# A conditional block's first sequences copied in DRAM, updated there by indirect transfers, and loaded once

## The chip, the cores and the metric

The kernel runs on one core of a Trainium2 chip. A core has five engines that run side by side, each with its own instruction stream: TensorE (PE, matrix products), VectorE (DVE), ScalarE (ACT), GpSimd (POOL) and SyncE (SP, which here only issues DMA transfers). Sixteen DMA engines move the data; transfers are issued from the queues of SP, ACT and POOL. The metric is the device time of one launch in microseconds (us).

## The reference

The input is `x` (32 sequences of 128 tokens of 512 features, float32), a conditioning vector per sequence, and a mask that is true only at the tail of a sequence (0 to 32 of its 128 tokens).

```python
shift, scale, gate_msa = jnp.split(_silu(t) @ ada_w + ada_b, 3, axis=1)
norm = _layernorm(x) * (1.0 + scale[:, None]) + shift[:, None]
norm = jnp.where(m, norm, 0.0)
fwd = _ssm_fallback(norm, ssm_w1, ssm_b1, ssm_w2, ssm_b2)   # gelu(u @ w1 + b1) @ w2 + b2
bwd = ...                                                   # the same with bwd_*, token by token
x = x + gate_msa[:, None] * jnp.where(m, fwd + bwd, 0.0)
shift_mlp, scale_mlp, gate_mlp = jnp.split(_silu(t) @ ffada_w + ffada_b, 3, axis=1)
ff_norm = _layernorm(x) * (1.0 + scale_mlp[:, None]) + shift_mlp[:, None]
h = _gelu(ff_norm @ ff_w1 + ff_b1)                          # 512 -> 1024
return x + gate_mlp[:, None] * (h @ ff_w2 + ff_b2)
```

The first half changes only masked tokens, some 512 of the 4096. The second half is a feed-forward layer over all tokens.

## The kernel before, in words

**Slots.** The masked tokens are numbered in order; these numbers are slots. The kernel finds the token of each slot on the chip (`find_slots`, `tokens_of`), gathers the rows of `x` for 512 slots, 128 at a time, into the tiles `xc` (`gather_slots`, L232), and runs the first half on these rows alone, in two parts of 256 slots. For each part it modulates (L167, L168), transposes on PE and copies the result with ACT (`transposed_slots`, L175, L176), multiplies by the first weights with a Gelu on ACT (`hidden`, L184, L188), and multiplies by the second (`project`, L198). `finish_slots` adds the bias, multiplies by the gate, adds the slot's row of x (L200, L201, L289) and stores 128 finished rows to a DRAM buffer `x1_rows` (L290). The hidden steps and projects of the first part are called "s0", of the second "s1"; the four finishes are numbered 0 to 3.

**Pairs.** The second half takes the sequences in four pairs of sides; a side is 4 sequences, a pair is 1024 tokens. The x of a pair is loaded by four transfers of two sequences each (`load_side`, L319). Then `take_first_half` (L656) overwrites the masked tokens' rows in these tiles by eight indirect transfers from `x1_rows`, issued by POOL, one for each sequence. For each token the statistics are taken (`Statistics`, L688, L689; the root is POOL's L694), x is normalised (L700), transposed to features by rows, and scaled and shifted (`scale_and_shift`: L708 on DVE, L710 on ACT). In the first pair, side 0 is transposed in blocks of 32 by DVE (L1132) and by 16 transfers that put the blocks in place, 8 from SP's queue and 8 from ACT's (`turned`, L727); side 1 is transposed by PE (`transposed`, L716) in four groups called turn(0) to turn(3), which stand between and behind the matmuls of project "s3".

**Seven products instead of eight.** Both feed-forward products are done by a recursive block scheme with seven block products, P1 to P7, in place of eight. It needs sums and differences of blocks: of tokens (`TokenBlocks.one(1..4)`, L757; `token_sums`, L817 to L827, all on DVE), and of weights. `weight_sums(1..4)` (L577) forms the combinations of ff_w1 on DVE, in two buffers that they use in turn: the tiles `spare`, which later hold x of the second pair, for 1 and 3, and `t_2` for 2 and 4. Each is stored to the DRAM buffer `t_rows` by transfers from SP's queue (L579, L581, L582); the product loads them as `tw` when it needs them (L834). `fw2_of.combine(0..3)` (L308) forms combinations of ff_w2. `FirstProduct` works through outer products 1, 2, 5, 6, 3, 7, 4; its matmuls are L888, `seed` (L932 on DVE, L934 on ACT) prepares an accumulator with earlier results, and P6, P7 and P4 end with additions on DVE (L913, L918, L923), some also with POOL's additions L939, L968 and L972. `SecondProduct` follows (L1068).

**What sets the order.** The whole part up to L1320 is a manual schedule: every engine runs its instructions exactly in the order of the program text, and waits only at semaphores. So a step that waits holds back all that its engine has behind it. Around the change the program is: first part of slots, `weight_sums(1)` and (2), finish 0, the "s3" transposes, finish 1, the modulation of the second half (`mod2`, its transposes L618, `modT` L621), `weight_sums(3)` and (4), then the first pair's x, "s1", and finishes 2 and 3. Finishes 2 and 3 belong to slots of later pairs.

The tile pool `xp` has eight places: two `xc` pairs, two `spare` and the four x tiles of a pair.

## Time and profile before

| | |
|---|---|
| time, median of 3 runs | 470.43 us (468.70 to 472.58) |
| the profiled execution's own time | 470.92 us |
| its span, first to last instruction | 469.2 us |
| PE busy | 452.4 us (96%), 2000 matmuls |
| DVE busy | 334.0 us (71%), 538 instructions |
| ACT busy | 174.9 us (37%) |
| POOL busy | 159.4 us (34%) |
| granted TensorE clock, mean | 0.995 |
| moved by DMA | 70.41 MB, mean 150 GB/s |

Busy time doesn't tell what bounds a stage; waits and the order of time do. A timeline line has the start, the duration, the engine, the line of the program, what is written and read, and in brackets how long the engine was idle before it and what ended that. A line of waits has the total, the number and the longest. A line of the stages has the busy time of PE, PE's weight loads, DVE, ACT and POOL (with the instructions in brackets), then the granted clock, the busy share of the DMA engines and their GB/s.

### The profile page before, as it was taken

Reading aid. Unit: us, or ns where it says so; the run is one execution under the profiler, and the core shown is the slowest. Engines: PE = TensorE matmul, PEld = TensorE weight load, DVE = VectorE, ACT = ScalarE, POOL = GpSimd, SP = SyncE. Lnnn points to the kernel's source line nnn. Section 1 sums busy time; section 2 is a strip of 40 time slices with the busy share of each in tenths; the row PEclk is TensorE's granted clock in tenths of the full one; section 3 lists DMA queues with packets and bytes.
Section 4 is the critical chain, followed back from the end, with each engine's and each line's share of the span. In section 5 each row is a group of like instructions: output and inputs, shape, how many; then the busy total and the mean of one; then the engine's idle time right before and its main releaser. Section 6 shows DMA issues by size and latency. Waiting matters only on the chain.

```text
span 469.2 us, 5826 instructions
## 1 busy us (share of the span) xinstructions
PE 452.4 (96%) x2000; PEld 365.3 (78%) x2000; DVE 334.0 (71%) x538; ACT 174.9 (37%) x380; POOL 159.4 (34%) x151
## 2 busy tenths in 40 slices
PE   6899999897999999999999999999999999999995
PEld 2475384475878888888888888888888888888884
DVE  4649377999778966997687498967873995434645
ACT  3131022543365074153643712545537134462000
POOL 6200063046876000189740003897100024660000
PEclk9999999999999999999999999999999999999999
DMA  8999943490413861854068528240863341213012
GB/s 278 386 408 362 394 172 53 86 345 19 121 44 134 137 90 49 312 174 163 1 194 106 106 98 288 102 161 3 217 100 88 125 168 62 96 64 117 0 76 107
DMA packets 82194, 70.41 MB, mean 150 GB/s; under 512 B 63136, under 2 KB 63664, under 8 KB 81138
## 3 DMA queue, kind: packets, MB, share of 16 engines
q1 hardware_dynamic: 67298, 57.95, 40.1%
q0 software_dynamic: 4256, 10.75, 6.8%
q10 hardware_dynamic: 10608, 1.32, 2.0%
q8 instruction: 17, 0.28, 0.2%
q14 instruction: 15, 0.12, 0.1%
HBM read 56.83 MB, written 13.17 MB: 149 GB/s over the span
## 4 chain that ended last, share of the span: by engine, by line
PE 61%; POOL 6%; ACT 6%; DVE 5%; issue 2%; POOLq 0%; DVEq 0%
PE a_o L1068 18%; PE e_o L1068 16%; PE a_m L888 14%; PE e_m L888 12%; ACT hb L850 2%; POOL hb L972 2%; ACT ha L850 1%; POOL ha L972 1%; POOL ha L939 1%; POOL rstd L694 1%; DVE xT L827 1%; PE last L1068 1%; DVE sx L817 1%; ACT a_o L1014 1%; ACT e_o L1014 1%
## 5 line engine op out<-in xcount | busy, mean ns | idle before, releaser
L939 POOL TENSOR_TENSOR ha<-p_m,ha 128x512 f32<-128x512 f32 x20 | 27.2, 1361 | 152.7 <-ACT ha L946 143.4
L1068 PE MATMUL e_o<-fw,ha 128*128 128x256 f32 x256 | 57.9, 379 | 0.0
L710 ACT ACTIVATE xT<-xT,modT 128x128 f32<-128x128 f32 x104 | 41.0, 480 | 40.2 <-DMA xT<-xn 39.7
L1068 PE MATMUL a_o<-t,hb 128*128 128x256 f32 x240 | 54.1, 379 | 0.0
L1068 PEld LDWEIGHTS e_o<-fw,ha 128*128 128x128 f32 x256 | 48.6, 190 | 6.6
L1068 PEld LDWEIGHTS a_o<-t,hb 128*128 128x128 f32 x240 | 45.6, 190 | 6.2
L656 POOL DMA_INDIRECT x<-x_rows,slot_i x32 | 36.6, 1144 | 30.2 <-DMA x_rows<-t_s 21.3
L850 ACT ACTIVATE hb<-hb,biasT 128x256 f32<-128x256 f32 x64 | 29.0, 500 | 29.9 <-POOL hb L972 19.3
L939 POOL TENSOR_TENSOR hb<-p_m,hb 128x512 f32<-128x512 f32 x20 | 29.8, 1489 | 18.2 <-DVE hb L918 17.9
L902 ACT COPY p_m<-e_m 128x512 f32<-128x512 f32 x27 | 15.8, 585 | 50.4 <-PE e_m L888 47.1
L946 ACT COPY ha<-e_m 128x512 f32<-128x512 f32 x32 | 18.5, 577 | 30.6 <-PE e_m L888 28.6
L1068 PE MATMUL e_o<-fw,s 128*128 128x256 f32 x128 | 29.2, 381 | 0.5 <-DVE s L1022 0.4
L1068 PE MATMUL a_o<-fw,ha 128*128 128x256 f32 x128 | 29.0, 380 | 0.0
L1068 PE MATMUL a_o<-t,s 128*128 128x256 f32 x128 | 28.9, 379 | 0.0
L184 PE MATMUL ph_s<-xT_s,w 128*128 128x256 f32 x128 | 28.7, 382 | 0.0
L198 PE MATMUL po_s<-w,h_s 128*128 128x512 f32 x64 | 28.5, 592 | 0.0
L1068 PEld LDWEIGHTS e_o<-fw,s 128*128 128x128 f32 x128 | 24.1, 190 | 4.9 <-DVE s L1022 1.7
L184 PEld LDWEIGHTS ph_s<-xT_s,w 128*128 128x128 f32 x128 | 24.0, 190 | 4.7 <-ACT h_s L188 1.5
L1068 PEld LDWEIGHTS a_o<-fw,ha 128*128 128x128 f32 x128 | 24.2, 190 | 3.5 <-ACT a_o L1014 0.2
L1068 PEld LDWEIGHTS a_o<-t,s 128*128 128x128 f32 x128 | 24.3, 190 | 3.3
L913 DVE TENSOR_TENSOR e_m<-a_m,ha 128x512 f32<-128x512 f32 x20 | 13.9, 696 | 17.1 <-POOL ha L939 6.6
L850 ACT ACTIVATE ha<-e_m,biasT 128x256 f32<-128x256 f32 x48 | 20.0, 467 | 14.9 <-PE e_m L888 9.6
(206 smaller groups left out, 878.1 us busy)
## 6 DMA issues: line engine op xcount, KB each, us to landing
tw<-t_rows SPq DMA_DIRECT2D x16, 896.0 KB, 5.2
x<-in_x_dram SPq DMA_DIRECT2D x16, 512.0 KB, 9.3
gate<-gate_rows POOLq DMA_DIRECT2D x8, 1024.0 KB
out_dram<-x SPq DMA_DIRECT2D x15, 512.0 KB, 3.1
xT<-xn SPq DMA_DIRECT2D x92, 64.0 KB, 2.7
fw<-in_L_cond_ff_w_dram SPq DMA_DIRECT2D x2, 2048.0 KB
ada_f<-in_L_cond_ffada_w_dram SPq DMA_DIRECT2D x4, 768.0 KB, 13.6
ada_a<-in_L_cond_ada_w_dram SPq DMA_DIRECT2D x4, 512.0 KB, 5.5
```

The costliest lines, as they stand in the source:

```text
L184: nc.tensor.matmul(ph[:, :n], w[:, k, ts(f, P)], xT[:, k, :], start=(k == 0), stop=(k == KC - 1))
L198: nc.tensor.matmul(po, h[f][:, ts(i, P)], w[:, f, :], start=(f == 0), stop=(f == HC - 1))
L656: nc.gpsimd.indirect_dma_start(out=xs[i // G][i % G // 2][:, i % 2], out_offset=None, in_=x1_rows[:slots, :], in_offset=bass.IndirectOffse ...
L710: nc.scalar.activation(out, src, AF.Identity, bias=shift, scale=scale)
L850: nc.scalar.activation(dst[:, n], src[:, n], AF.Gelu_apprx_tanh, bias=biasT[:, f : f + 1])
L888: nc.tensor.matmul(bank[:, ts(n, QT)], self.w_block(j, product)[:, ts(n, P)], self.x_block(j, product), start=(product in ("P1", "P5") and ...
L902: nc.scalar.copy(p5, e)
L913: nc.vector.tensor_tensor(e, a, p5, add)
L939: nc.gpsimd.tensor_tensor(self.place(RESULT[j], c), self.p5[j], other, ALU.add)
L946: nc.scalar.copy(self.place(RESULT[j], c), src)
L972: nc.gpsimd.tensor_tensor(part, self.place("21", c), part, ALU.add)
L1068: nc.tensor.matmul(part, src[:, k, ts(i, P)], w[product][:, k, :], start=(last and k == 0), stop=True, skip_group_check=True,)
```

## The change

The x of the first pair is no longer loaded at once. A transfer from SP's queue copies its 1024 rows from `x` to a DRAM buffer `x0_rows`, at the place where the four loads stood. Finishes 0 and 1 (slots 0 to 255) each issue, besides the old store, an indirect transfer from POOL that writes the finished rows to their tokens' rows in `x0_rows`; rows whose token isn't in the first pair are dropped by the bound. After finish 1 the four loads of x follow, from `x0_rows`. The eight indirect transfers of `take_first_half` for the first pair are gone. To mark empty slots, an unused slot's token number is now put beyond the bound (`FAR`), so the gathers get a bound too, and the two tile pairs for the slots are zeroed beforehand; the loop for further slots at the end of the program is adapted in the same way.

The order changes with it. `weight_sums(3)` and (4) stand between finishes 0 and 1; all stores to `t_rows` are issued from ACT's queue instead of SP's. `fw2_of.combine(0, 1)` stands before the first pair's statistics instead of in the second-next windows of the products. Two statistics of side 1 stand before the normalising of side 0. Seven of the eight hidden steps of "s1" stand before the block transfers of side 0, the eighth behind them. All of side 0 is scaled by ACT, all of side 1 by DVE from PE's transposes. turn(0) stands inside project "s2", turn(1) to turn(3) inside the first half of project "s3". The token blocks 1 to 3 stand before the additions of finish 3, and block 4 behind them; token sums of product 1 are spread between the phases of products 1 and 2.

```diff
-    def project(i, h, w, bias, gate, name, between=None):
+    def project(i, h, w, name, between=None):
...
+        return po
+
+    def gated(po, bias, gate, name):
+
+        t = tp.tile([P, D], F32, tag="t", name=f"t_{name}")
         nc.vector.tensor_tensor(t, po, bias, ALU.add)
         nc.vector.tensor_tensor(t, t, gate, ALU.mult)
...
-        nc.vector.tensor_tensor(token_i, token, view[:, :, S - 1], ALU.add)
+        nc.vector.scalar_tensor_tensor(
+            token_i, token, FAR, view[:, :, S - 1], ALU.add, ALU.add
+        )
...
+    def scatter(src, token_col, rows, n):
+
+        nc.gpsimd.indirect_dma_start(
+            out=rows,
+            out_offset=bass.IndirectOffsetOnAxis(ap=token_col, axis=0),
+            in_=src,
+            in_offset=None,
+            bounds_check=n - 1,
+            oob_is_err=False,
         )
...
     def finish_slots(at, h1, gate, between=None):
-        t = project(at % (NC // 2), h1, w2, b2, gate, f"s{at}", between)
+        keep_slots(at, project(at % (NC // 2), h1, w2, f"s{at}", between), gate)
+
+    def keep_slots(at, po, gate):
+        t = gated(po, b2, gate, f"s_{at}")
         nc.vector.tensor_tensor(t, t, xc[at], ALU.add)
+        if at < NC // 2:
+            scatter(t, token_0[:, at : at + 1], x0_rows, 2 * G * S)
         nc.sync.dma_start(x1_rows[ts(at, P), :], t)
...
+        rows = x if p else x0_rows.rearrange("(b s) d -> b s d", s=S)
...
-            nc.sync.dma_start(t, x[b : b + 2].rearrange("b s d -> s b d"))
+            nc.sync.dma_start(t, rows[b : b + 2].rearrange("b s d -> s b d"))
...
+    slots_x = [xp.tile([P, 2, D], F32, tag="x", name=f"xc_{h}") for h in range(2)]
+    nc.vector.memset(slots_x[0], 0.0)
...
-    x_of = {0: load_x(0)}
+
+    x0_rows = dram.tile([2 * G * S, D], F32, name="x0_rows")
+    nc.sync.dma_start(x0_rows, x_rows[: 2 * G * S])
...
-            nc.sync.dma_start(t_rows[j - 1], t_sum[j][0][:, :7])
+            nc.scalar.dma_start(t_rows[j - 1], t_sum[j][0][:, :7])
         else:
-            nc.sync.dma_start(t_rows[j - 1, :, :4], t_sum[j][0])
-            nc.sync.dma_start(t_rows[j - 1, :, 4:], t_sum[j][1][:, :3])
+            nc.scalar.dma_start(t_rows[j - 1, :, :4], t_sum[j][0])
+            nc.scalar.dma_start(t_rows[j - 1, :, 4:], t_sum[j][1][:, :3])
...
     finish_slots(0, h1, gs[0])
+    weight_sums(3)
+    weight_sums(4)
     transposed_slots(xn_s[1], xT_t[:, :, ts(1, P)], "s3")
     nc.vector.tensor_scalar(modb_f[B : 2 * B], modb_f[B : 2 * B], 1.0, None, ALU.add)
     finish_slots(1, h1, gs[1])
+    x_of = {0: load_x(0)}
...
-    weight_sums(3)
-    weight_sums(4)
...
-    take_first_half(0, x_of[0], range(G + 2))
     gate_rows = dram.tile([B, D], F32, name="gate_rows")
     nc.gpsimd.dma_start(gate_rows, mod2[2 * B : 3 * B, :])
-    h1 = hidden(xT_t, NH, w1, 0, AF.Gelu, "s1", ssm)
-    nc.scalar.activation(warm, biasT[0:1, 0:1], AF.Gelu_apprx_tanh)
     fw2_of = Weights(fw2, HC // 2, D // 2, t_2)
+    fw2_of.combine(0, 1)
...
     stats[0].root()
-    take_first_half(0, x_of[0], range(G + 2, 2 * G))
+    stats[1].one(0)
+    stats[1].one(1)
...
+    h1 = hidden(xT_t, NH, w1, 0, AF.Gelu, "s1", ssm, range(HC - 1))
     turned(xn, xT[0], (nc.sync, nc.scalar))
-    for k in range(KC // 2, KC):
+    h1 += hidden(xT_t, NH, w1, 0, AF.Gelu, "s1", ssm, range(HC - 1, HC))
+    nc.scalar.activation(warm, biasT[0:1, 0:1], AF.Gelu_apprx_tanh)
+    for k in range(KC):
         scaled(0, xT[0], k)
-    for i in range(G):
-        stats[1].one(i)
+    stats[1].one(2)
+    stats[1].one(3)
     stats[1].root()
...
-    finish_slots(2, h1, gs[0])
...
+    finish_slots(2, h1, gs[0], {6: turn(0)})
+    po = project(1, h1, w2, "s3", {0: turn(1), 2: turn(2), 4: turn(3)})
     of_x[0] = TokenBlocks(0, xT)
     for j in (1, 2, 3):
         of_x[0].one(j)
+    keep_slots(3, po, gs[1])
+    of_x[0].one(4)
...
+    now.token_sums(1, 0)
     now.apart(1)
     now.do(1, "P1")
     now.seed(1)
     now.do(2, "P1")
     now.do(1, "P2", "P5", "P6")
-    of_x[0].one(4)
+    now.token_sums(1, 1)
...
-    for n in range(4):
-        now.token_sums(1, n)
+    now.token_sums(1, 2)
+    now.token_sums(1, 3)
...
-                put(4, 1, fw2_of.combine, 0)
-                put(5, 1, fw2_of.combine, 1)
```

More of the change, by code (lines that the diff above doesn't have):

```diff
@@ L198, in project @@
             nc.tensor.matmul(po, h[f][:, ts(i, P)], w[:, f, :], start=(f == 0), stop=(f == HC - 1))
-        t = tp.tile([P, D], F32, tag="t", name=f"t_{name}_{i}")
+        return po
+    def gated(po, bias, gate, name):
+        t = tp.tile([P, D], F32, tag="t", name=f"t_{name}")
         nc.vector.tensor_tensor(t, po, bias, ALU.add)
@@ L236, in gather @@
             in_offset=bass.IndirectOffsetOnAxis(ap=token_col, axis=0),
+            bounds_check=T - 1,
+            oob_is_err=False,
+        )
+    def scatter(src, token_col, rows, n):
[5 more added lines that the diff above has]
+            bounds_check=n - 1,
+            oob_is_err=False,
         )
@@ L245, in gather_slots @@
     def gather_slots(token_i):
-        both = xp.tile([P, 2, D], F32, tag="x", name=f"xc_{len(xc)}")
+        both = slots_x[len(xc) // 2]
         for c in range(NC // 2):
@@ L407 @@
         pattern=[[0, 1]],
-        base=0,
+        base=-int(FAR),
         channel_multiplier=S,
@@ L457 @@
     nc.scalar.activation(warm, s_sb[0:1, 0:1], AF.Gelu)
-    token_i = find_slots(0)
-    gather_slots(token_i)
+    token_0 = find_slots(0)
+    gather_slots(token_0)
     for j, w in enumerate((ssm_w1, bwd_w1)):
@@ L475 @@
     pick_slots(1)
+    nc.vector.memset(slots_x[1], 0.0)
     slot_of = ssm.tile([B, S], F32, name="slot_of")
@@ L647, with take_first_half @@
     nc.vector.tensor_tensor(fb2_step, fb2[:, D // 2 :], fb2[:, : D // 2], ALU.subtract)
-    weight_sums(3)
-    weight_sums(4)
-    def take_first_half(p, xs, which=range(2 * G)):
-        slots = NH if p == 0 else NS
+    def take_first_half(p, xs, which):
+        slots = NS
         for i in which:
@@ L710, in scale_and_shift, with transposed @@
             nc.scalar.activation(out, src, AF.Identity, bias=shift, scale=scale)
-    def transposed(g, xn, xT, k, by_vector):
+    def transposed(g, xn, xT, k):
         ptr = ps_t.tile([P, 512], F32, tag="tr", name=f"ptr_{g}_{k}")
@@ L717, in transposed @@
         for i in range(G):
-            scale_and_shift(xT[:, k, ts(i, P)], ptr[:, ts(i, P)], k, g * G + i, by_vector)
+            scale_and_shift(xT[:, k, ts(i, P)], ptr[:, ts(i, P)], k, g * G + i, True)
     def turned(xn, xT, queues):
@@ L727, in turned, with scaled @@
                 queues[b % len(queues)].dma_start(dst[ts(q, R), b], src[ts(b, R), q])
-    def scaled(g, xT, k, by_vector=False):
+    def scaled(g, xT, k):
         for i in range(G):
             t = xT[:, k, ts(i, P)]
-            scale_and_shift(t, t, k, g * G + i, by_vector)
+            scale_and_shift(t, t, k, g * G + i, False)
     def new_xT(p, side):
@@ L1143 @@
             xn_b.append(stats[1].normalised(2 * c + i, both[:, i]))
-    finish_slots(2, h1, gs[0])
     def turn(k):
-        transposed(1, xn_b, xT[1], k, by_vector=k < KC // 2)
-    def turn_and_scale(k):
-        turn(k)
-        scaled(0, xT[0], k, by_vector=True)
-    finish_slots(
-        3,
-        h1,
-        gs[1],
-        {3: lambda: turn_and_scale(0), 5: lambda: turn_and_scale(1), 7: lambda: turn(2)},
-    )
-    turn(3)
+        return lambda: transposed(1, xn_b, xT[1], k)
+    finish_slots(2, h1, gs[0], {6: turn(0)})
+    po = project(1, h1, w2, "s3", {0: turn(1), 2: turn(2), 4: turn(3)})
     of_x[0] = TokenBlocks(0, xT)
@@ L1348 @@
             tok_i = tokens_of(pick_l, col_l, 1, "l", lp)
-            none = stp.tile([P, 1], F32, tag="none", name="none", bufs=1)
-            nc.vector.tensor_scalar(none, col_l, total, FAR, ALU.is_ge, ALU.mult)
-            to_i = stp.tile([P, 1], I32, tag="to_i", name="to_i", bufs=1)
-            nc.vector.tensor_tensor(to_i, none, tok_i, ALU.add)
             xl = lp.tile([P, D], F32, name="xl")
+            nc.vector.memset(xl, 0.0)
             gather(xl, tok_i)
@@ L1377 @@
                 gate_l = of_slots(pick_l, 0, mod, 2, ps_h, "h", f"gate_l{half_no}")
-                t = project(0, h_l, wb, bias, gate_l, f"l{half_no}")
+                t = gated(project(0, h_l, wb, f"l{half_no}"), bias, gate_l, f"l{half_no}")
                 nc.vector.tensor_tensor(xl, xl, t, ALU.add)
-            nc.gpsimd.indirect_dma_start(
-                out=out_rows,
-                out_offset=bass.IndirectOffsetOnAxis(ap=to_i, axis=0),
-                in_=xl,
-                in_offset=None,
-                bounds_check=T - 1,
-                oob_is_err=False,
-            )
+            scatter(xl, tok_i, out_rows, T)
             nc.vector.tensor_scalar(row_l, row_l, float(P), None, ALU.add)
```

## The prediction

> **What bounds the kernel now.** I read the page's busy times first: TensorE (PE) is busy 452.4 of 469.2 us, so a change gains only where PE idles, and loses wherever it idles longer. The waits of PE say where (total us, times, longest).
>
> ```profile
> PE e_m L888 <- DVE e_m L932: 2.7, 2, 2.4
> PE e_m L888 <- ACT e_m L934: 1.3, 1, 1.3
> PE a_m L888 <- DVE hb L918: 1.1, 2, 0.8
> ...
> PE e_o L1068 <- DVE s L1022: 0.4, 2, 0.2
> ```
>
> The same list from 139 us on holds only its last line, 0.4 us: what is late at 139 us is late at the end. So the case is decided between 40 and 139 us. PE in order of time there (start, us):
>
> ```profile
> 82.38 1.60 PE L716 MATMUL ptr<-ident,xn 128*128 128x128 f32 x4 [0.45 <-DVE xn L700]
> ...
> 93.43 1.13 PE L888 MATMUL e_m<-xT,fw 128*128 128x256 f32 x4 [1.25 <-ACT e_m L934]
> ...
> 115.72 1.66 PE L888 MATMUL e_m<-xn_sy,tw 128*128 128x256 f32 x4 [2.40 <-DVE e_m L932]
> 117.17 1.91 PE L888 MATMUL a_m<-xn_sy,tw 128*128 128x256 f32 x4
> 118.87 1.39 PE L888 MATMUL a_m<-sx,tw 128*128 128x256 f32 x4
> ```
>
> A group of 4 matmuls takes 0.864 us from start to start. The 46 groups from 89.96 to 139.40 should take 39.7 us and take 49.4: 9.7 us are lost, 1.75 more before 89.96. The largest loss is at 115.72: 2.40 us idle, then three groups at a lower clock (4.38 us for 2.59: 1.8 lost). Who is late there, the chain of waits says: VectorE (DVE), which works without a break from the first pair's statistics.
>
> ```profile
> 111.78 2.94 DVE xT L827
> 114.72 0.33 DVE s L827
> 115.05 0.62 DVE e_m L932
> 115.67 0.04 issue
> 115.72 1.66 PE e_m L888 x4
> ```
>
> This DVE run begins with the first pair's x. Its third tile arrives at 69.07, and side 0 is normalised and block-transposed at 77.05, which I call T:
>
> ```profile
> 69.07 0.69 DVE L688 BATCH_NORM_STATS2 st<-x 128x6 f32<-128x512 f32 x1 [1.62 <-DMA x<-x_rows,slot_i]
> ...
> 76.41 0.71 DVE L1132 STREAM_TRANSPOSE xn<-xn 128x512 f32<-128x512 f32 x1
> 77.05 0.65 DVE L688 BATCH_NORM_STATS2 st<-x 128x6 f32<-128x512 f32 x1
> ```
>
> From T to the seed at 115.72 it takes 38.7 us. Last, the stages, for the DMA engines (last two columns: share, GB/s):
>
> ```profile
> 54.00:56.00 2.00, 2.00 (x16) 0.48 (x10) 0.66 (x1) 0.00 (x0) 0.00 (x0) 1.00 1.06 436
> 56.00:58.00 2.00, 2.00 (x6) 0.75 (x7) 0.69 (x1) 0.67 (x2) 0.00 (x0) 1.00 0.98 397
> 58.00:60.00 2.00, 2.00 (x13) 1.71 (x13) 1.40 (x8) 0.50 (x1) 0.00 (x0) 1.00 0.30 111
> ```
>
> The engines are full until 58, at 385 to 436 GB/s. The packet records show the order: the 2.1 MB of fw2 from about 42 to 47.5, x to 53, then the t_rows writes.
>
> **What the skill says.** "DMA: Bandwidth & Descriptors", Queues, rings and completion order: each DMA engine takes its rows (SP's queue, ScalarE's, GpSimd's) in turn, packet by packet. The trace agrees: at 26 to 28 us GpSimd's gather got 83 packets of 4096 bytes beside 106 of SP's. Same page, Anatomy of one DMA: about 2.0 us are fixed, most of it the receipt of the write; here a 256 KB row store took 2.0 at least. "TensorE: Matmul & The Clock Gate", Part 1: after an idle window of about 3.4 us the clock is halved until PE has been busy as long; the dip after 115.72 is of this kind. "SBUF — State Buffer", Who interferes with whom: a DVE operation with two SBUF inputs and a GpSimd one that reads SBUF exclude each other; L827 took 2.94 us for its usual 0.68 while GpSimd (POOL) ran two L939.
>
> **The change, part by part.** Small ones first. Two zeroed 128x1024 slot tiles: 1.23 us each at most (L308, same size), in DVE's wait of 1.70 us for the mask and in its wait of 2.01 before 12.08; uncovered they would cost PE's start up to 0.5. Bounds on the gathers and the fused add: nothing, the instructions stay. The tail loop doesn't run (the trace has no line of it). Eight gathers L656 leave POOL, 1.1 + 0.3 us each, off the path but for their data. The two fw2 combinations at 122.73 and 129.41 move into DVE's wait for x (2.5 us); PE's 0.84 wait at 132.39, behind the second, goes.
>
> *Queues.* The six t_rows issues move from SP to ScalarE (ACT), 0.32 to 1.17 us each, and wait there for DVE. Behind them stands the copy of the "s3" transposes (45.57 before), which PE needs at 58.41. weight_sums(3) and (4), 4.3 us of DVE, move from 60.52 to behind finish_slots(0) (end 47.5), and write the tiles that the first two t_rows writes still read. Those 0.92 MB writes now share the engines with fw2 (2 KB packets against their 3 to 7 KB, so they get 60 to 78%): the first lands at about 47.5, the second at 50.8. So (3) runs 47.5 to 49.7, (4) 50.9 to 53.1, finish_slots(1) ends at 55.7 (54.65 before); mod is ready at 56.4 for transposes that PE begins at 57.8. The cover is 1.4 us; every later us stalls PE.
>
> *The copy in DRAM* stands behind fw2 in SP's queue, where the four x loads stood (landed by 53). By its end the engines have moved fw2 2.1, the copy 2.1 and some 3.5 of the four t_rows writes, 3.2: 7.4 MB from 41.9 at 0.40 MB/us is 18.5 us, so 60.4, and 1.0 for the receipt: **61.4**. No row shows a copy from DRAM to DRAM. Bounds: 54.5 if it were served as the x loads were, with no write ahead; 67 at half the rate. I take the full rate, since the stores and loads of the trace both reach it.
>
> *The scatters* replace nothing on this path: each waits for the copy, and the second for the first. Nearest row, the gather: 1.05 us on POOL, then 2.7 (2.5 to 3.45 here) to landing, 3.8 with the semaphore; under full queues a gather of the opening took 7 from issue. Two: **69.0**. Behind them on POOL are only gate_rows and the two roots, which are later.
>
> *The loads.* Two 0.52 MB tiles: 0.1 + 2.0 + 1.05/0.385 = 4.8, so side 0 is there at **73.8** instead of 69.07. Then DVE: two statistics 1.8, variance 0.2, two of side 1 1.75 (over the 1.2 of POOL's root), normalising and transposing 4.95: T = **82.5**, 5.45 later. The x1_rows stores that remain on SP ahead of the tw loads now end with finish_slots(3), T + 20.7, and tw lands 5.3 later, T + 26.2; PE wants it at T + 26.5. Nothing, but without slack.
>
> *From T on.* The 16 transposes and scales are the same in number: DVE now takes 16 from PSUM, 5.4 us (4.9 before), ACT 16 of 0.40, 6.4 (6.05). The last Gelu of "s1" now stands behind ACT's eight block transfers, 6.66 us in issue, so PE's last step of project "s2" waits until T + 7.4. PE reaches turn(0) at 77.6 and idles some 10 us to T + 5.05; before it had 0.45. DVE: scales of turn(0) T + 7.0; finish 2, with po ready at T + 8.6, T + 10.8; turns 1 to 3 (1.36 each) 14.9; blocks 1 to 3 18.6; finish 3 20.7; block 4 21.9. Then 12 sums of 0.6, 4 of 0.34 and 8 results of 0.6, 13.4, the 4.1 that the POOL overlaps cost before (2.26 + 0.85 + 0.99), and 0.6 of waits: seed at **T + 40**. PE, from T + 17.0 with 25 groups of 0.864, is there at T + 38.6, so it waits little and keeps its clock.
>
> *Sum.* Seed at 122.5 against 115.72 + 1.8 of slow matmuls = 117.5: +5.0; less 0.84: +4.1. On the profiled execution's 470.92 (span 469.2 and 1.7 around) that is 475.0; this execution is 0.5 above the median of 470.43, so **474.5**.
>
> **The rivals.** *The copy is early.* Its 32 rows of 64 KB are large packets and might take the engines from the writes; for it speaks that turn-taking goes by packets, against it that fw2 is still ahead and loses its turns to the writes. Copy at 54.5, T = 75.6, seed 115.6: -1.9 - 0.84 gives 467.7, **faster**. It decides from a copy landed at 57.3 (T = 78.4). *The writes are late instead:* ScalarE's issues might wait behind SP's as in the run before, where t_rows landed 10.8 us after issue. Then weight_sums(3) waits to 56.5, finish_slots(1) ends at 63.2 and PE stalls 6 us at the transposes of mod; second scatter 67.1, T = 80.6, 472.7. For it: SP's four x loads took 3.76 us to issue at that place, so issuing does back up; against it, SP and ACT issued their block transfers side by side from 77.2. *DRAM is slow:* the copy at half rate (67), or scatters that land as the opening's gather did: T = 88, 480. For it: a copy both reads and writes DRAM; against it, the stores alone reach 436 GB/s, and the queues are nearly empty by the scatters. That the change doesn't do what it says is excluded: its instruction order has the eight gathers gone and the scatters between copy and loads.
>
> **How the numbers follow.** Likeliest case 0.48, early copy 0.17, late writes 0.13, slow DRAM 0.22. About 1% (4.7 us) is what a measurement of this kernel can tell from no change. The likeliest case, itself 471 to 478 by the landing times, lies half on each side of 475.1; of the early copy a third is beyond 465.7. Faster 0.06, within 1% 0.47, slower 0.47. The range 467.5 to 481 takes in the early copy's time and the half-rate copy.
>
> **What would show it.** Right: the first statistics of x after 73, TensorE idle for 8 us or more before the transposes at about 78, no 2.4 us wait at the seed of product 6, copy landing near 61. Wrong: statistics of side 0 before 68, or a wait of PE at the transposes of mod (the late writes). The forecast fails most easily at the copy's landing: each us of it is a us of the end.

## The result, and the profile after

The changed kernel takes **482.0 us** (median of 4 runs, 481.04 to 483.17), the kernel before 470.9 beside it: ratio **1.024** (95% interval 1.021 to 1.028), slower. That is above the forecast of 474.5 and 1 us above its range. The profiled execution took 481.36 us (span 479.3), where the steps gave 475.0.

Three marks divide it: T, when side 0 is normalised and turned; P1, when TensorE starts the first product; E, when its first 46 groups are done (start of `a_o<-fw,ha`, 139.40 before). What follows E, to the end of the launch, is equal within 0.4 us. The lines of the marks P1 and E, before and then after:

```profile
89.96 1.10 PE L888 MATMUL a_m_alone<-xT,fw 128*128 128x256 f32 x4
139.40 3.62 PE L1068 MATMUL a_o<-fw,ha 128*128 128x256 f32 x16
```

```profile
104.20 1.03 PE L920 MATMUL a_m_alone<-xT,fw 128*128 128x256 f32 x4
150.16 3.62 PE L1100 MATMUL a_o<-fw,ha 128*128 128x256 f32 x16
```

| us | before | forecast | after | after less forecast |
|---|---|---|---|---|
| T | 77.05 | 82.5 | 85.13 | +2.6 |
| T to P1 | 12.91 | 17.0 | 19.07 | +2.1 |
| P1 to E | 49.44 | 44.1 | 45.96 | +1.9 |

(Forecast of the last row: seed at 122.5, and from the seed to E before's 139.40 - 117.5 less 0.84.) The three misses add up to 6.6 us; the profiled time misses the forecast by 6.4.

The waits of TensorE after (total us, times, longest). The 2.7 us for DVE's L932 (L964 here) are down to 1.0, but of these five lines only the second was there before at its length:

```profile
PE ptr L748 <- DVE xn L732: 8.0, 1, 8.0
PE pb L450 <- DVE mask_f L445: 3.3, 1, 3.3
PE e_m L920 <- DVE e_m L945: 1.7, 2, 1.4
PE a_m L920 <- DVE t_s L204: 1.6, 1, 1.6
PE ptr_mod L652 <- DVE mod L283: 1.1, 1, 1.1
```

The chain of the first pair's x after (start us, length): indirect write, second indirect write, loads, statistics, turn.

```profile
64.37 1.05 DMA x_rows<-t_s,token_i_s
...
68.90 2.75 DMA x_rows<-t_s,token_i_s
...
71.67 3.70 DMA x<-x_rows
...
75.40 0.70 DVE st L720
...
85.21 0.59 DVE st L720
```

The copy's completion is counted at 63.5, and the first indirect write starts 0.85 us later. From the landing to T it takes 21.6 us; the forecast had 21.1, from 61.4. And TensorE from its long wait past the seed of product 6 (126.14; no wait there, where before had 2.40):

```profile
88.82 1.76 PE L748 MATMUL ptr<-ident,xn 128*128 128x128 f32 x4 [7.97 <-DVE xn L732]
93.01 2.07 PE L198 MATMUL po_s<-w,h_s 128*128 128x512 f32 x2 [0.73 <-ACT h_s L188]
...
106.80 1.10 PE L920 MATMUL a_m<-xT,fw 128*128 128x256 f32 x4 [1.57 <-DVE t_s L204]
126.14 1.13 PE L920 MATMUL e_m<-xn_sy,tw 128*128 128x256 f32 x4
139.42 1.13 PE L920 MATMUL e_m<-s,fw 128*128 128x256 f32 x4 [1.37 <-DVE e_m L945]
```

By stages (PE busy, its loads, DVE, ACT, POOL, then granted clock, DMA share, GB/s), two stretches stand out. From 42 to 46 the DMA engines are full, to 48 at 0.78, and yet they move 226 to 258 GB/s; the kernel before moved 343 to 402 there. From 84 to 96 TensorE is granted half its clock; before, 1.00. After:

```profile
42.00:44.00 2.00, 2.00 (x6) 0.94 (x5) 2.00 (x4) 0.00 (x0) 0.00 (x0) 1.00 1.00 258
44.00:46.00 2.00, 2.00 (x9) 1.09 (x8) 1.71 (x4) 0.00 (x0) 0.00 (x0) 1.00 1.02 231
46.00:48.00 2.00, 2.00 (x6) 0.82 (x5) 1.97 (x4) 0.00 (x0) 0.00 (x0) 1.00 0.78 226
...
84.00:88.00 4.00, 0.00 (x0) 0.00 (x0) 2.86 (x8) 0.00 (x0) 0.92 (x1) 0.50 0.30 39
88.00:92.00 4.00, 3.18 (x6) 1.16 (x6) 3.29 (x8) 0.00 (x0) 0.09 (x1) 0.50 0.99 145
92.00:96.00 4.00, 3.27 (x8) 1.85 (x8) 0.77 (x2) 2.37 (x5) 0.00 (x0) 0.50 0.53 78
```

Before:

```profile
44.00:46.00 2.00, 2.00 (x9) 1.15 (x8) 1.97 (x3) 0.43 (x1) 0.00 (x0) 1.00 1.05 402
...
84.00:88.00 4.00, 4.00 (x15) 1.99 (x15) 3.86 (x11) 1.06 (x3) 0.00 (x0) 1.00 0.65 138
```

### The profile page after: what moved, and what is told of

Same layout as the page of the kernel before. It is cut to its first block, busy times and chain, and to the rows that moved or that the text cites. A ratio compares the mean times of both kernels' runs of the same rounds, so it can differ in the third digit from the quotient of the medians.

```text
span 479.3 us, 5814 instructions
## 1 busy us (share of the span) xinstructions
PE 455.7 (95%) x2000; PEld 367.2 (77%) x2000; DVE 333.5 (70%) x540; ACT 175.4 (37%) x380; POOL 152.5 (32%) x145
## 4 chain that ended last, share of the span: by engine, by line
PE 64%; POOL 6%; ACT 6%; DVE 4%; issue 3%; DMA 2%; ACTq 1%; POOLq 0%; DVEq 0%
PE a_o L1100 18%; PE e_o L1100 15%; PE a_m L920 15%; PE e_m L920 13%; POOL hb L1004 2%; ACT hb L882 2%; POOL ha L971 1%; PE po_s L198 1%; POOL rstd L726 1%; ACT ha L882 1%; DVE st L720 1%; POOL ha L1004 1%; POOL x L688 1%; DMA xT<-xn 1%; DMA x_rows<-t_s,token_i_s 1%
## 5 line engine op out<-in xcount | busy, mean ns | idle before, releaser
L742 ACT ACTIVATE xT<-xT,modT 128x128 f32<-128x128 f32 x112 | 44.2, 480 | 29.0 <-DMA xT<-xn 28.9
L971 POOL TENSOR_TENSOR hb<-p_m,hb 128x512 f32<-128x512 f32 x20 | 27.8, 1389 | 25.7 <-DVE hb L950 25.3
L198 PE MATMUL po_s<-w,h_s 128*128 128x512 f32 x64 | 31.5, 636 | 0.7 <-ACT h_s L188 0.7
L688 POOL DMA_INDIRECT x<-x_rows,slot_i x24 | 28.9, 1204 | 8.3 <-issue 7.8
L184 PE MATMUL ph_s<-xT_s,w 128*128 128x256 f32 x128 | 30.1, 395 | 0.0
L184 PEld LDWEIGHTS ph_s<-xT_s,w 128*128 128x128 f32 x128 | 25.0, 198 | 5.0 <-ACT h_s L188 1.5
## 6 DMA issues: line engine op xcount, KB each, us to landing
ada_f<-in_L_cond_ffada_w_dram SPq DMA_DIRECT2D x4, 768.0 KB, 16.4
```

What stands on the lines that cost most here:

```text
L184: nc.tensor.matmul(ph[:, :n], w[:, k, ts(f, P)], xT[:, k, :], start=(k == 0), stop=(k == KC - 1))
L198: nc.tensor.matmul(po, h[f][:, ts(i, P)], w[:, f, :], start=(f == 0), stop=(f == HC - 1))
L688: nc.gpsimd.indirect_dma_start(out=xs[i // G][i % G // 2][:, i % 2], out_offset=None, in_=x1_rows[:slots, :], in_offset=bass.IndirectOffse ...
L742: nc.scalar.activation(out, src, AF.Identity, bias=shift, scale=scale)
L971: nc.gpsimd.tensor_tensor(self.place(RESULT[j], c), self.p5[j], other, ALU.add)
```

## The experiments

Theory 1, the prediction's: the late x of the first pair costs the time. Rivals: the early weight sums and their stall of TensorE (2); the new order behind T (3); a late issue of the copy (4); indirect writes that are slow wherever the copy is (5). For parts of the miss: TensorE's clock (6), the early combine (7), GpSimd's gathers (8), a block of results finished late (9). I started by undoing one part each, and then built the change up from the kernel before.

### Undoing one part

**No copy in DRAM** (loads and eight gathers as before, all else changed):

```diff
-    nc.sync.dma_start(x0_rows, x_rows[: 2 * G * S])
+    x_of = {0: load_x(0)}
...
+    take_first_half(0, x_of[0], range(G + 2))
```

> The changed kernel without its copy in DRAM: the first pair's x is loaded straight from the input where the copy was issued, and the first half's results come into it by eight row gathers, as in the kernel before; all else (early weight sums, order of turn and scale) stays as changed. Theory 1 (the late x of the first pair costs the time: copy, two scatters in a row, loads): the first side's x is whole when the last of its gathers lands, some 7 us earlier than 75.4 us, T (side 0 turned) falls from 85.1 to about 77 to 78, and the time from 482 to 472 to 475 us. Theory 2 (the early weight sums and their stall of TensorE cost it): the modulation still waits for the weight sums, hidden layer s1 starts at 60.3 as now, and the time stays within 2 us of 482. Theory 3 (order of the vector and scalar work behind T costs it): T moves but the products start at T + 19 or later and the time is 476 to 479.

Measured: 475.4 us, ratio 1.0125 (1.0095 to 1.0155). T = 81.92, not 77 to 78: VectorE's fourth weight sum waited 6.3 us for a store of the staging rows, the results of slots came out at 63.2 in place of 54.7, and the gathers began at 66.07 (60.80 before). So 5 of T's 8 us stay without any copy: x is late here too, for another reason. Theory 1 in its simple form, that the copy is what makes it late, falls.

**Late weight sums**, and **stores on SyncE**:

```diff
     finish_slots(0, h1, gs[0])
-    weight_sums(3)
-    weight_sums(4)
...
     nc.vector.tensor_tensor(fb2_step, ...)
+    weight_sums(3)
+    weight_sums(4)
```

> The changed kernel with the weight sums of blocks 3 and 4 put back behind the bias step, so that VectorE's modulation row is not queued behind them. Theory 1 (late x): the 1.1 us wait of TensorE for the modulation goes, and with less traffic ahead of it the copy lands 3 to 5 us earlier (59 to 61 us), so T is about 80 and the time 476 to 478 us. Theory 2 (weight sums and the stall): the time falls to 473 or below. Theory 4 (the copy is late because its issue is late, and not because of traffic): the copy lands at 63 to 64.5 as now, T stays near 85, and the time within 1.5 us of 482.

Measured: 481.6 us, ratio 1.024 (1.021 to 1.027), as with them early. The stall for the modulation goes, but SyncE's issue of the copy now waits 5 us for a store (47.02 in place of 42.44), the copy lands at 63.0 (63.5 in the changed kernel) and T is 85.79. Undoing the part alone brings nothing.

```diff
-            nc.scalar.dma_start(t_rows[j - 1], t_sum[j][0][:, :7])
+            nc.sync.dma_start(t_rows[j - 1], t_sum[j][0][:, :7])
```

> The changed kernel with the stores of the weight sums' staging rows issued by SyncE again in place of ScalarE. Theory 4 (moving these stores to ScalarE's queue moved later transfers' completion counters, so that SyncE waits for an unrelated load ahead of the bias broadcasts): the broadcast that is issued at 32.75 us is issued 3 us or more earlier again, the copy is issued near 39 in place of 42.4. But the stores now stand behind SyncE's issues, so the weight sums, and VectorE's modulation row behind them, come 5 to 8 us later and TensorE waits 6 to 7 us for the modulation: T near 84, time 480 to 482 us. Without theory 4 (the issue of the copy stays at 42 or later) the late modulation comes on top and the time is 485 us or more.

Measured: **475.1 us**, ratio 1.012 (1.009 to 1.015): 7 us of the 11 lie in the choice of this queue. The stall for the modulation is 4.55 us, where 6 to 7 were expected, and costs nothing, since x is later still. I had expected that stall to eat the gain. GpSimd's indirect writes and TensorE in this run:

```profile
54.51 1.05 POOL L249 DMA_INDIRECT x_rows<-t_s,token_i_s  x1 [15.05 <-DMA x_rows<-in_x_dram]
63.12 0.99 POOL L249 DMA_INDIRECT x_rows<-t_s,token_i_s  x1 [7.55 <-DVE t_s L311]
```

```profile
63.48 0.90 PE L652 MATMUL ptr_mod<-ident,mod 96*128 96x96 f32 x4 [4.55 <-DVE mod L283]
88.44 1.12 PE L198 MATMUL po_s<-w,h_s 128*128 128x512 f32 x2 [1.73 <-ACT h_s L188]
97.59 1.03 PE L920 MATMUL a_m_alone<-xT,fw 128*128 128x256 f32 x4
```

The copy lands 10 us earlier (the first write starts at 54.51 against 64.37), and the second write waits for the slots' result, no longer for the copy; T = 80.56. The packet records say how: here the copy's 32 packets of 64 KB run from 46.6 to 53.2, in the changed kernel from 55.3 to 62.9. The load of fw2, behind which the copy stands, takes 10.3 us from its issue to its landing here and took 16.3 there. There ScalarE's queue got 2.5 MB through between 42 and 56 and SyncE's 2.5, where here SyncE's alone gets 5.6. The 2 KB packets of SyncE's queue took 176 ns in the mean there at 42 to 46 us; they take 94 here and 89 before.

Theory 4 holds for a smaller part. Only the stores' queue differs between the two runs, and the issue of fw2 moves from 41.56 to 38.47, 3.1 of the 9.8 us between the two landings of the copy (that of the copy moves from 42.44 to 40.66). SyncE's waits (total, times, longest) show why, ahead of the bias broadcasts; after:

```profile
SPq L119 <- DMA ada_f<-in_L_cond_ffada_w_dram: 6.8, 3, 3.4
```

with the stores on SyncE:

```profile
SPq L119 <- DMA ada_f<-in_L_cond_ffada_w_dram: 3.1, 2, 1.6
```

The broadcasts have no data in common with these loads. What they share is the completion counter, the semaphore that counts a transfer's landing: by the semaphore numbers in the traces, each of these issues waits for the counter that it will use itself, and which an earlier load holds until it lands. With the stores on SyncE, the first broadcast of the modulation's bias uses counter 103 and goes at 25.35. In the changed kernel 103 and 106 are passed over there; ScalarE's first two stores use them. The broadcast gets 104, which the load of fw holds until 32.67, and goes at 32.75; the issues behind it, that of the copy included, come 1.8 to 4.0 us later.

**The copy ahead of fw2**, with the sums late, and by itself:

```diff
-    nc.sync.dma_start(fw2, ff_w2.rearrange("(k p) f -> p k f", p=P))
-
     x0_rows = dram.tile([2 * G * S, D], F32, name="x0_rows")
     nc.sync.dma_start(x0_rows, x_rows[: 2 * G * S])
+    nc.sync.dma_start(fw2, ff_w2.rearrange("(k p) f -> p k f", p=P))
```

> The changed kernel with the weight sums of blocks 3 and 4 late, and the copy in DRAM issued ahead of the load of fw2 rather than behind it. Theory 1 (late x, bounded by the landing of the copy): the copy lands near 53 us, before the first slot result is ready (56 us or so), the scatters start at once, the loads are issued at about 65 and T is 75 to 77; the time 469 to 472 us, at the kernel before. Theory 3 (order behind T costs it): T moves as said, but the time stays above 474. Theory 5 (indirect writes and loads behind the copy set T whatever the copy does): T stays above 80.

Measured: 478.3 us, ratio 1.019 (1.012 to 1.026). The copy landed near 54 as expected, but the second indirect write was issued only 7.2 us after the first, beside fw2's traffic, and took some 6.9 more until the loads; T = 82.58, and the products began at T + 19.9.

> The changed kernel with one line moved: the copy in DRAM is issued ahead of the load of fw2, not behind it; weight sums early and their stores on ScalarE's queue, as changed. If the copy's landing decides T (as the prediction has it), it lands near 54 to 56, the second block of results (58.7) now decides the second indirect write, T falls from 85.1 to 77 to 80 and the time to 473 to 478. If fw2, which now comes later, holds the weight or modulation work in its place, or the indirect writes are slow beside it, T stays above 82 and the time above 479.

Measured: 476.9 us, ratio 1.011 (1.007 to 1.015): 5 us off. The first indirect write goes at 52.55, the second at 60.91, when the slots' result is there; T = 80.50. So the landing decides T down to the result of the second block of slots, and no further.

### The change built up, one edit at a time

Each row adds one edit to the row above; the last is the whole change.

| | ratio to before | T | T to P1 | P1 to E |
|---|---|---|---|---|
| before | | 77.05 | 12.91 | 49.44 |
| + x's path through DRAM | 0.998 (0.995 to 1.001) | 75.55 | 13.30 | 49.14 |
| + new order of turns, scales, token sums | 1.012 (1.006 to 1.018) | 77.53 | 19.01 | 47.58 |
| + combine ahead of the statistics | 1.033 (1.028 to 1.038) | 88.21 | 19.48 | 45.94 |
| + weight sums early | 1.012 (1.009 to 1.015) | 80.56 | 17.03 | 45.96 |
| + their stores on ScalarE's queue | 1.024 (1.021 to 1.028) | 85.13 | 19.07 | 45.96 |

**The path alone**, in the kernel before:

```diff
-    x_of = {0: load_x(0)}
+    nc.sync.dma_start(x0_rows, x_rows[: 2 * G * S])
...
+        if at < NC // 2:
+            scatter(t, token_0[:, at : at + 1], x0_rows, 2 * G * S)
...
     finish_slots(1, h1, gs[1])
+    x_of = {0: load_x(0)}
...
-    take_first_half(0, x_of[0], range(G + 2))
```

> The kernel before with only the new path of the first pair's x: copied in DRAM, the two blocks of results put into it by indirect transfers, then loaded; weight sums, their stores, turns and scales stay as before. Theory 1 (this path by itself costs the time): the first side is whole 5 us or more later than before, T is 82 or later and the time 475 or more. Theory 2' (the path by itself is as good as the eight gathers; what makes it late is the company of the early weight sums and their stores): the copy lands near 54 us, the indirect writes go at about 54.5 and 58.5, the loads at 63, the first side's x is there at 67, T is 76 to 78, and the time 469.5 to 472.

Measured: 470.7 us, no difference that can be told. The first indirect write goes at 54.55, the second at 60.28, the first statistic starts at 66.14, as the first of the four tiles lands, and T is 1.5 us **earlier** than with the gathers:

```profile
66.14 0.69 DVE L712 BATCH_NORM_STATS2 st<-x 128x6 f32<-128x512 f32 x1 [0.60 <-DMA x<-x_rows]
75.55 0.65 DVE L712 BATCH_NORM_STATS2 st<-x 128x6 f32<-128x512 f32 x1
```

The path by itself doesn't cost the time; theories 1 and 5 fall.

**The order.** The next row was made from the changed kernel with late weight sums and their stores on SyncE, as above, by putting the combine of fw2 back into the product's windows:

```diff
-    fw2_of.combine(0, 1)
...
+                put(4, 1, fw2_of.combine, 0)
+                put(5, 1, fw2_of.combine, 1)
```

> As the run with late sums and their stores on SyncE, but the combine of fw2's halves is no longer ahead of the first pair's statistics: it is back in the first product's windows, as in the kernel before. What stays of the change is the path of x through DRAM and the new order of turns, scales and token sums. Theory 7 (in that run the combine, waiting for the staging tile's store, held the statistics back, so that the early combine is what needs the early sums): the first statistic starts near 66 us in place of 78.5, T is 75 to 76, the products start at T + 17 to T + 19.5, that is 93 to 95, they take 46 to 47.5 us to the last of the first 46 groups, and the time is 470.5 to 473.5. If the early combine is not what held them: T near 88 and 485 again.

Measured: 476.4 us. The statistic starts at 66.26, as theory 7 says, but T is 77.53 (a statistic of side 1 ahead of side 0's turn waits 1.44 us for its own tile), and the products begin at T + 19.0 and are only 1.6 us shorter. Theory 3 holds: the new order costs 5.8 us between the two profiled executions (476.76 - 471.0), with x on time, nearly all of it between T and P1 (19.01 in place of 13.30). Some 2.2 us of this are TensorE's half clock, an estimate: from its restart to P1 it takes 11.36 us here and 9.15 at full clock (next section). The rest lies in the turns, the scales and the Gelu behind the block transfers, which no run takes apart.

The order without the path is the run without a copy, with the two edits of "late weight sums" and "stores on SyncE" added:

> Only the new order of turns, scales and token sums behind the first pair's x, as changed: x comes as in the kernel before (direct loads and eight row gathers), the weight sums of blocks 3 and 4 stand behind the bias step again, and SyncE issues the stores of their staging rows. Theory 3 (the new order behind T costs the time): side 0 is turned at T = 79 to 80 (the statistics now stand behind the early combine), the products start at T + 17 or later in place of T + 12.9 in the kernel before, and the time is 475 us or more. Theory 1 (the path of x and the sums ahead of it cost nearly all): the products' start moves 4 us later but they are 3.5 us shorter, and the time is 471 to 473.

Measured: 477.3 us, ratio 1.013 (1.007 to 1.018), with x by gathers, the sums late and the combine early. T is 82.43, later than expected, again from the combine, which waited to 70.28 for a staging store.

**The combine and the sums.** With the combine early and the sums late (the two edits above, in the changed kernel):

> The changed kernel with both the weight sums late and their stores on SyncE's queue; the copy in DRAM, the indirect writes and the new order stay. If traffic of the staging rows beside the copy is what made it land late (theory 1 in its second form: with stores on ScalarE's queue the copy shares the transfer engines with them), it lands near 53.7 us as it did with the stores on SyncE, the two indirect writes go at about 54.5 and 58.5, the loads at 62 to 63, T is 76 to 78 and the time 472 to 474. If the early weight sums themselves cost nothing (only their stores do), T is 80.5 again and the time 475.

Measured: **485.9 us**, the slowest run of all and far from what I expected. The x was there as before, but VectorE stood at the combine, which writes the buffer `t_2` that the last weight sum's store still reads; the statistics, queued behind it, started at 78.48:

```profile
64.39 0.95 DVE L608 TENSOR_TENSOR t<-t,t 128x768 f32<-128x768 f32 x1
76.08 1.23 DVE L332 TENSOR_TENSOR t<-fw 128x1024 f32<-128x1024 f32 x1 [10.74 <-issue]
...
78.48 0.69 DVE L720 BATCH_NORM_STATS2 st<-x 128x6 f32<-128x512 f32 x1
```

("issue" is no releaser that the view shows. The store's landing is counted at 76.00, and with the sums early or the combine late the wait is gone.) So the parts lean on each other: the early combine needs the early sums, these need their first stores landed, which on SyncE's queue stand behind the copy, and on ScalarE's go beside it and delay it.

### The clock after a long wait

In both runs whose clock stays at 1.00 from 84 to 100 us (stores on SyncE; no copy), TensorE takes 9.15 and 9.14 us from its restart after the last Gelu of "s1" to P1. In the changed kernel it takes 11.19 (93.01 to 104.20), in the others of this order without a fill 10.8 to 12.0, with the same instructions. To test it, unread transposes fill the wait of 8 us:

```diff
         ptr = ps_t.tile([P, 512], F32, tag="tr", name=f"ptr_{g}_{k}")
+        for i in range(48 if g == 1 and k == 0 else 0):
+            nc.tensor.transpose(ptr[:, :P], ident, ident)
```

> The changed kernel, all of it, with 48 transposes of the identity added on TensorE ahead of the first turn of side 1, into the tile that this turn then overwrites: they fill the wait of 8.0 us for VectorE's xn with work that nobody reads. Theory 6 (TensorE is granted half its clock for some 9 us after that wait, and the turns and the last projection run at half speed): the four transposes take 0.6 to 1.1 us in place of 1.76, the granted clock stays near 1.0 from 84 to 98 us, the products start 1.5 to 2.5 us earlier and the time is 479 to 480. Otherwise (the delay from T to the products is the scalar engine's block transfers and its last activation): start and time do not move, 481 to 482.

Measured: 479.0 us, ratio 1.017 (1.012 to 1.022), but T to P1 only from 19.07 to 18.74: a further wait for the Gelu brought the half clock back at 92 (0.65 from 92 to 96). The second version fills both waits:

```diff
+    def fill_and_turn():
+        fill(60)()
+        turn(0)()
+
-    finish_slots(2, h1, gs[0], {6: turn(0)})
+    finish_slots(2, h1, gs[0], {6: fill_and_turn, 7: fill(14)})
```

> The changed kernel, with unread transposes of the identity on TensorE in both of its waits ahead of the products: 60 ahead of the first turn of side 1 (wait of 8.0 us) and 14 ahead of the last step of the third projection (wait of 0.7 to 1.8 us). Theory 6 (half clock after the wait): the granted clock stays above 0.95 from 84 to 100 us, the turns take 0.6 us and the four-matmul steps of the projection 1.88 throughout, the products start at T + 17.0 to T + 17.5 in place of T + 19.1, and the time is 478 to 480. Otherwise: the clock stays up but the products start at T + 18.7 or later.

Measured: 478.4 us, ratio 1.015 (1.011 to 1.019).

```profile
84.00:88.00 4.00, 1.67 (x16) 1.43 (x14) 2.76 (x7) 0.00 (x0) 1.01 (x1) 1.00 0.45 64
88.00:92.00 4.00, 3.63 (x9) 1.75 (x10) 2.92 (x8) 0.00 (x0) 0.00 (x0) 0.57 0.96 140
92.00:96.00 4.00, 3.65 (x22) 2.45 (x20) 0.95 (x2) 2.40 (x5) 0.00 (x0) 1.00 0.45 63
```

From the restart (93.78) to P1 (102.93) it takes 9.15 us again: the 2.04 us are the clock. (The 0.57 is a mean: the clock records have half clock from 88.5 to 91.9.) T to P1 is 18.3, not 17.0 to 17.5, since ScalarE's eight block transfers took 8.45 us to issue in this run (7.20 after), and the Gelu behind them came 1.3 us later; 2.66 us of wait were left, too, and the clock dipped behind them. Between the two profiled executions (2.7 us), T makes 0.5 us, T to P1 0.8, P1 to E 2.9 (43.06, for the reason that the next run shows), and 1.4 is lost behind E.

### The products

**No gathers** of the second pair in the first product (its first six sequences go without the first half's result):

```diff
-            put(2 if p == 0 else 1, 6, take_first_half, p + 1, x_next, range(G))
-            put(2, 6, take_first_half, p + 1, x_next, range(G, G + 2))
+            if p:
+                ...
```

> The changed kernel without the six row gathers that put the first half's results into the x of the second pair's first six sequences: that part of the computation is left out. Theory 8 (GpSimd's gathers, late and slow beside VectorE, hold back its sums, on which VectorE and TensorE wait, in the first product): the waits of 0.31, 0.44 and 1.37 us of TensorE for VectorE's e_m between 131 and 140 us go, 46 groups end 2 to 3 us earlier, the time is 478.5 to 480.5. If these waits have another cause they stay and the time is 481 to 482.5.

Measured: 478.1 us, ratio 1.016 (1.009 to 1.022); P1 to E 42.88 in place of 45.96, and the three waits are gone. In the changed kernel, GpSimd's gathers and the sum behind them, for which VectorE waits:

```profile
121.78 2.43 POOL L688 DMA_INDIRECT x<-x_rows,slot_i  x1 [0.30 <-issue]
124.52 1.83 POOL L688 DMA_INDIRECT x<-x_rows,slot_i  x1 [0.30 <-ACT p_m L934]
...
128.97 1.27 POOL L971 TENSOR_TENSOR ha<-p_m,ha 128x512 f32<-128x512 f32 x1
```

Two of them take 2.43 and 1.83 us where others take 1.0 to 1.5. The five runs of this order with a gather of 2.43 us (the changed kernel, stores on SyncE, that with late sums, that with late sums and late combine, and the copy ahead by itself) have P1 to E at 45.9 to 47.6; the two fills, whose gathers take 1.0 to 1.4, have 43.1, the others 43.1 to 44.8. In all five the slow gather starts 17.6 us behind P1; in the others the third gather starts at 16.4 to 17.4 us, or at 17.8. So it goes with how the engines' work falls together; what in that makes it slow isn't settled.

**The fourth block of results ahead of the token blocks:**

```diff
+    keep_slots(3, po, gs[1])
     of_x[0] = TokenBlocks(0, xT)
     for j in (1, 2, 3):
         of_x[0].one(j)
-    keep_slots(3, po, gs[1])
```

> The changed kernel with the fourth block of results finished on VectorE ahead of the first three token blocks, not behind them. TensorE's wait of 1.57 us at the second group of P1 is for that block's accumulator to be read. Theory 9 (this wait costs its length): it goes, nothing takes its place, the time is 480 to 481. Rival: the token blocks come 2 us later and a wait of the same size stands at one of the next groups; 481.5 to 482.5.

Measured: 479.1 us, ratio 1.019 (1.012 to 1.026). The wait of 1.57 is gone, and waits of 0.60, 0.19 and 1.49 stand at the next groups, as the rival says. The 2.9 us gained go with two other things: T is 1.0 us earlier, and no gather takes longer than 1.5 us. Theory 9 isn't supported.

**Only the places of token sums and the fourth token block**, in the kernel before; then with x's path; then with that block and the first sum behind the first group of products:

```diff
         of_x[0].one(j)
+    of_x[0].one(4)
...
+    now.token_sums(1, 0)
     now.apart(1)
...
     now.do(1, "P2", "P5", "P6")
-    of_x[0].one(4)
+    now.token_sums(1, 1)
```

> The kernel before with only the fourth token block and side 1's token sums in the changed places; x comes as before. If these places gain by themselves: the wait of 2.4 us at the seed of product 6 and the half clock behind it go, 46 groups take 46 to 47 us in place of 49.4, the time is 467.5 to 469.5. If only together with the path through DRAM: 470 to 471.5.

> The kernel before with two parts of the change: the path of x through DRAM (as in the run of that alone, 470.7 us) and the new places of the fourth token block and of side 1's token sums. Turns, scales, weight sums, their stores and the combine stay as before. If the 3.5 us that the products are shorter in the changed kernel come from these places, the wait of 2.4 us for VectorE's e_m at the seed and the half clock behind it go and the time is 467.5 to 469. If they come from the turns and scales being out of VectorE's way, the start of the products is late by what is put ahead of it, 2.7 us, and the time is 470 to 473.

> As the run of the kernel before with x's path and the token sums' places, 468.3 us, but with the fourth token block and the first token sum behind the first four groups of products rather than ahead of them. If the 1.49 us wait of TensorE for VectorE's e_m near 97 us is due to these two standing ahead of it: it goes and the time is 466.5 to 468. If a later sum then comes late: 468 to 470.

Measured: 469.0, 468.3 and 468.7 us; ratios 0.996 (0.993 to 0.998), **0.995** (0.993 to 0.997) and **0.993** (0.990 to 0.996). All three beat both kernels, the kernel before by 0.4 to 0.7%. The wait of 2.4 us at the seed is gone, and P1 to E is 46.5 in the first and second (49.4 before). In the kernel with the path as well, the seed of product 6 (112.55) has no wait:

```profile
97.77 1.13 PE L912 MATMUL a_m_alone<-xT,t 128*128 128x256 f32 x4 [1.49 <-DVE e_m L937]
112.55 1.13 PE L912 MATMUL e_m<-xn_sy,tw 128*128 128x256 f32 x4
```

A wait of 1.49 us at 97.77 is left. In the third run it stands as before (1.49 at 98.70): VectorE has no work of that first group, so the edit left its order as it was, and this run is a second look at the one before. Its expectation tested nothing. With the places alone as good within the intervals, the path's 1.5 us of T are not resolved in the time.

## Why the prediction was wrong

The sign of its likeliest case was right and its size was not: +4.1 us where +10.4 came. Three terms of its sum were too small: the copy's landing (63.5 for 61.4), TensorE's matmuls behind its long wait (2.0 us of half clock, charged at full clock), and the products (1.9 us, waits that begin at GpSimd's gathers). By its steps:

- **What bounds it** (PE's waits between 40 and 139 us; nothing after): right, the time behind E differs by 0.3 us.
- **Queues.** The stores landed later than said: the third sum ended at 52.0 (49.7), the fourth began at 53.9 (50.9), finish 1 ended at 58.7 (55.7), and TensorE stalled 1.1 us behind a cover of 1.4. Mis-sized by 3 us, without weight in the end: the run with 4.55 us of that stall was 7 us faster.
- **The copy in DRAM** is the first term that failed. It was sized as 7.4 MB at 0.40 MB/us from 41.9. The copy itself ran near the rate taken (27 of its packets, 1.8 MB, ended between 58 and 62), but from 42 to 48 us 0.24 MB/us were moved, 1.0 MB or 2.5 us short. The term's own lesson is larger: it took the company as given. With the stores behind the copy on its own queue it lands 10 us earlier.
- **The scatters and loads**: 3.8 for each scatter forecast, 4.5 and 2.8 measured; 4.8 to the second load's landing forecast, 5.1 measured; T less the landing right within 0.5 us.
- **From T on.** T + 17.0 for P1 is what full clock gives (17.03 with the stores on SyncE). It failed because the step let TensorE idle for 10 us and then charged its matmuls at full speed, though the prediction had quoted the Trainium skill, "TensorE: Matmul & The Clock Gate", Part 1, for just this. The trace agrees with the page: half clock from 84 to 96, which costs 2.04 us.
- **DVE's 4.1 us of overlaps with GpSimd** were carried over from before, but not who waits for GpSimd in the new order: its gathers hold its sums, these VectorE's, these TensorE. Without the gathers P1 to E is 3.1 us shorter. The wait for finish 3 behind the token blocks (1.57) was overlooked; in the run without it, waits of 2.3 us in all stand at the next groups.
- **The rivals.** "The copy is early" did not come to pass as a whole; its price (T down, time down) was tried and is right in kind: 5 us. "The writes are late" would have been the better kernel, 475.1, since late sums stall only a TensorE that waits anyway. "DRAM is slow" came closest in time (480) for the wrong reason.
- **That the sum's gain is in the order**, 5.3 us of shorter products against 4.1 of a later start, is the deeper fault: the order was taken as a whole. Its sums' places give 3 us (P1 to E in the last three runs); its turns, scales and Gelu, with the half clock behind the wait, take 5.7.
- **Readings of the kernel before.** At 26 to 28 us GpSimd's gather got 90 packets beside 99 of SyncE's, not 83 beside 106. The engines did not move 385 to 436 GB/s all the way to 58: at 42 to 44 they moved 343, and at 40 to 42, also full (1.07), 230. The writes' 60 to 78% of the engines was an estimate; ScalarE's queue got 53% of the bytes at 42 to 46. And the 2.0 us of the row store are all of its time, so they don't measure a fixed part.

## What to carry to other kernels

When a change moves several things, find which of them need each other, and price each at the place where the other left it: here an early combine needed early sums, and the queue chosen for the stores of these delayed the very transfer that the change was about, while the path itself cost nothing. Moving a store to another engine's queue was not free here although that engine was idle: the stores then competed with transfers that they used to stand behind, and it cost 7 us. And a forecast that lets TensorE wait for many microseconds has to charge the half clock behind that wait: 2 us here behind 8.

## What the runs showed of the hardware

- A copy from DRAM to DRAM of 2.1 MB went as 32 packets of 65,536 bytes, most of them of 2.42 us; sixteen at once would be 0.43 MB/us, an estimate. From the first packet to the last it took 6.6 us behind fw2 on SyncE's queue (46.6 to 53.2).
- DMA engines that are full don't always move much: 258 and 231 GB/s at 42 to 46 us (shares 1.00 and 1.02) with two queues, where SyncE's queue alone made 343 and 402 in the kernel before. The mixture as such isn't it: it was at 332 to 340 GB/s from 43.5 to 44.5 and at 414 to 424 from 48 to 54. The slowest stretch, 45.5 to 46.5, has no data packet of ScalarE's queue in it; SyncE's 2 KB packets took 505 and then 331 ns in the mean there, and in the kernel before, SyncE's queue alone fell to 230 GB/s at 40 to 42. What makes these packets slow isn't settled.
- An issue can wait for a transfer that it has nothing to do with, through a completion counter that both use: the first bias broadcast waited until 32.75 for the load of fw (landed 32.67), and in the run with late sums the copy's issue waited 5.0 us for a store.
- Two indirect writes of 128 rows each to the same DRAM buffer: the second started 0.76 us after the first had landed, and so 4.5 us after the first in the changed kernel, 5.7 in the path alone, 7.2 beside fw2's traffic.
- In the clock records of these traces the clock is 1.00 or 0.50, and between 40 and 140 us a stretch at 0.50 lasts 3.41 us or a multiple of that (13.65 in the changed kernel). It doesn't take a long wait: 2.40 us (the kernel before) and 2.66 (the second fill) were followed by 3.41 us of half clock, 3.17 (the combine late) by 6.83, and in the copy ahead by itself 1.35 by 6.83, with four transposes behind it that took 1.61 us in place of 0.60. These waits are shorter than the idle window of about 3.4 us in the Trainium skill, "TensorE: Matmul & The Clock Gate", Part 1. The page calls that window free-running, so small gaps around such a wait may fill it; no run here separates that.
